# Cross-attention and mixture of experts: the second batch's last two tiles of the shared FFN, moved from in front of the experts to the stage of the gathers

## The chip, the cores and the metric

The kernel runs on one core of a Trainium2 chip. The metric is the device time of one launch in microseconds (us). All arithmetic is in fp32.

## The reference, cut to what matters

The input is 4 batches of 512 tokens with 512 features, so 2048 tokens, or 16 tiles of 128 tokens, 4 to a batch. A cross-attention block is added to the input; then comes a feed-forward block with 64 experts of which each token takes 6, and a shared feed-forward part that every token takes:

```
x = x + xattn(layernorm(x), context)
h = layernorm(x)
scores = softmax(h @ gate_w.T);  topk_w, topk_idx = top_k(scores, 6);  topk_w /= sum(topk_w)
# each expert takes up to 384 of the tokens sent to it
eo[e] = (silu(buf[e] @ w_gate[e].T) * (buf[e] @ w_up[e].T)) @ w_down[e].T      # 512 -> 352 -> 512
y[token] += topk_w * eo[expert, place]                                         # six rows a token
shared = (silu(h @ sh_gate.T) * (h @ sh_up.T)) @ sh_down.T                     # 512 -> 704 -> 512
out = x + y + shared
```

The change concerns `shared` and the sums over the six expert rows.

## The kernel before, in words

The result is kept in SBUF in `acc`, 16 tiles of 128 tokens by 512 features. The kernel runs in these stages, one after the other on TensorE:

1. Attention for the 16 tiles, with routing beside it. For every token the slots of its six expert rows go to `slot_get` and their weights to `top_w`. The normalised tokens go to DRAM twice, as rows (`h2_d`) and turned (`h2T_d`).
2. The shared FFN of batch 0 stands among the last routing steps of attention, with attention's buffers (`Here`).
3. The shared FFN of batch 1 follows in front of the experts, with the buffers of the later stages (`There`). Beside it the first experts' weights (`up_weights`, `down_weights`, issued by SyncE, called SP) and gathered tokens (`tokens`, issued by GpSimd, called POOL) are loaded.
4. 64 experts. The widths of the products depend on how many tokens an expert has (160, 192, 224, 256 or 384 columns; `kinds`, `by_width`). The results go to DRAM (`eo_d`).
5. The end: the shared FFN of batches 2 and 3 on TensorE, and beside it the sums. For each of 96 pairs of tile and rank, POOL gathers 128 rows of `eo_d` (`gather`, L873) and VectorE multiplies them by the weight and adds them to `acc` (`combine`, L884). A tile is written out (L865) when all has been added to it that is due in this stage (`added`, with its counter `left`).

`shared` is a generator: each `yield` ends a step, and the caller puts other work in between. Its first step loads the turned input of the batch into a slab (L122). Then come six slices of the 704 hidden features, five of 128 and one of 64. In a slice TensorE multiplies the gate's and the up's weights with the input (L128; the last slice has both in one product), ScalarE takes silu (L139) and VectorE multiplies (L140) into `hid`. A product over 512 features is four matmuls, and an fp32 matmul is two TensorE instructions in the trace, so a full slice has 16 and the last one 8. Then for each tile of the batch the down product (L145, twelve instructions) is added to `acc` (L148). There are eight slabs: six hold the shared weights, so two inputs fit at a time.

Products go to PSUM banks in pairs that are used in turn, `pg`, `pu`, `tx` and `pd`. The activations of the experts read a fixed 384 columns of a bank, also where the product wrote fewer.

In the end stage there are 12 buffers for gathered rows (`places`), so POOL can be 12 gathers ahead of the sums. The program's order fixes the rest: after each TensorE step of the shared FFN, VectorE's queue gets as many sums as bring the total to a share of 96, less a lag `behind` of 10 (5 after the last step; what is left then follows in a row). The share is counted in steps (`step` of `len(late) * slices`): six slices and four down tiles for each of two batches, 20 in all.

```
while done < NT * TOPK * step // (len(late) * slices) - (behind // 2 if last else behind):
    next(sums)
    done += 1
```

The order of PE, ACT, DVE and POOL instructions in the attention, expert and end stages is the program's order (`manual_schedule`); SP's order is arranged by the compiler.

Of the kernel before, what the change touches and what calls it, by code (L numbers as in the profile page):

```python
# [11 lines left out]
AF = mybir.ActivationFunctionType  # L12
ALU = mybir.AluOpType
AX = mybir.AxisListType

P = 128
B, S, D = 4, 512, 512
# [4 lines left out]
NT = B * S // P  # L22
TB = S // P
NC = D // P
E, F, TOPK = 64, 352, 6
# [6 lines left out]
FSC = [(i * P, min(P, FS - i * P)) for i in range((FS + P - 1) // P)]  # L32
# [1 line left out]
LN_EPS, QK_EPS = 1e-5, 1e-6  # L34
WIDTHS = (160, 192, 224, 256, CAP)
HALF = P // 2
BEFORE = 2
FAR = float(1 << 20)


# [1 line left out]
def xattn_moe_kernel(ctx, tc, a, out):  # L42
    nc = tc.nc
# [6 lines left out]
    h2T_d = dram.tile([D, B * S], F32, name="h2T_d")  # L50
# [3 lines left out]
    acc = keep.tile([P, NT, D], F32, name="acc")  # L54
# [40 lines left out]
    def slab(*shape):  # L95
        n = 1
        for m in shape:
            n *= m
        names = "abc"[:len(shape)]
        return slabs.tile([P, NC * D], F32, tag="slab", name="slab")[:, :n].rearrange(  # L100
            f"p ({' '.join(names)}) -> p {' '.join(names)}", **dict(zip(names, shape)))


    sh_gu, sh_down = [], []
# [10 lines left out]
            if full < 3:  # L115
                nc.sync.dma_start(sh_down[-1][:FS % P, full, :], a["sh_downT"][(f + full) * P:, :])

    def shared(b, get):


        xT = slab(NC, S)
        nc.sync.dma_start(xT, h2T_d.rearrange("(c p) n -> p c n", p=P)[:, :, b * S:(b + 1) * S])  # L122
        yield
        hid = [get.hid() for _ in range(0, len(FSC), 3)]

        def product(dst, w0):
            for c in range(NC):
                nc.tensor.matmul(dst, sh_gu[c][:, w0:w0 + P], xT[:, c, :], start=c == 0, stop=c == NC - 1)  # L128

        for fc, (f0, fn) in enumerate(FSC):  # L130
            pg, pu = get.pair()
            product(pg, f0)
            if fn == P:
                product(pu, FS + FS % P + f0)
            else:
                pu = pg[fn:]
            yield
            sg = get.sg()
            nc.scalar.activation(sg[:fn], pg[:fn], AF.Silu)  # L139
            nc.vector.tensor_tensor(hid[fc // 3][:fn, fc % 3, :], sg[:fn], pu[:fn], ALU.mult)  # L140
            yield
        for m in range(TB):
            pd = get.pd()
            for fc, (f0, fn) in enumerate(FSC):
                nc.tensor.matmul(pd, hid[fc // 3][:fn, fc % 3, m * P:(m + 1) * P], sh_down[fc // 3][:fn, fc % 3, :],  # L145
                                 start=fc == 0, stop=fc == len(FSC) - 1)
            t = b * TB + m
            nc.vector.tensor_tensor(acc[:, t, :], pd, acc[:, t, :], ALU.add)  # L148
            yield

    swp = ctx.enter_context(tc.tile_pool(name="swp", bufs=1))
# [4 lines left out]
    with ExitStack() as att:  # L156
# [425 lines left out]
        with tc.manual_schedule(engines=engines):  # L582
            new = scores(0, qTs[0], kvs[0][0])
            pr = w2.tile([P, NC, SC], F32, tag="pr", name="pr")
            for i in range(2):
                maximum(*new, i)
                exponentials(pr, *new, tail[0][2], 0, i)
            for u, (t, g) in enumerate(units):
                b, i = divmod(t, TB)
                pd, rd, sm = tail[t]  # L590
                if g == 0:
                    pc = ps_c.tile([P, NC, P], F32, tag="pc", name="pc")
                    if i == 2 and b + 2 < B:
                        load_batch(b + 2)
                    if t == NT - 2:
                        load_shared()
                mix_tail(pr, g, pd, rd, sm)
                if g == NC - 1:
                    wide = inverse_sums(sm)
                pr_u = pr  # L600
                if u + 1 < len(units):
                    tn, gn = units[u + 1]
                    new = scores(gn, qTs[tn], kvs[tn // TB][0])
                    pr = w2.tile([P, NC, SC], F32, tag="pr", name="pr")
                pT = [copied(turned(pr_u, c), nc.scalar) for c in range(2)]
                if u + 1 < len(units):
                    maximum(*new, 0)
                    maximum(*new, 1)
                    exponentials(pr, *new, tail[tn][2], gn, 0)
                beside()  # L610
                pT.append(copied(turned(pr_u, 2), nc.scalar))
                pT.append(copied(turned(pr_u, 3), nc.vector))
                if u + 1 < len(units):
                    exponentials(pr, *new, tail[tn][2], gn, 1)
                for c in range(2):
                    values(pc, g, c, pT[c], kvs[b][1])
                if g < NC - 1:
                    beside()
                for c in range(2, SC // P):
                    values(pc, g, c, pT[c], kvs[b][1])  # L620
                if g == NC - 1:
                    side.append(("finish", finish(t, pc, wide)))
                    beside()

            class Here:
                hid = staticmethod(lambda: w2.tile([P, NC, SC], F32, tag="pr", name="pr")[:, :3, :])
                sg = staticmethod(lambda: w2.tile([P, NC, P], F32, tag="pT", name="pT", bufs=5).rearrange(
                    "p a b -> p (a b)"))
                pair = staticmethod(lambda: (lambda ps: (ps[:, 0, :], ps[:, 1, :]))(
                    ps_s.tile([P, 2, SC], F32, tag="ps", name="ps")))  # L630
                pd = staticmethod(lambda: ps_s.tile([P, 2, SC], F32, tag="ps", name="ps")[:, 0, :])

            def advance(steps, n):
                for _ in range(n):
                    next(steps, None)

            (_, oldest), (_, older), (_, newer) = side
            advance(oldest, 1)
            work = shared(0, Here)
            next(work)  # L640

            for n_older, n_newer in ((5, 2), (4, 0), (0, 3), (0, 2), (0, 4), (0, 2)):
                next(work)
                advance(older, n_older)
                advance(newer, n_newer)
                next(work)
            advance(newer, 4)
            lists_made = plan()
            for _ in range(TB):
                next(lists_made, None)  # L650
                next(work)
            for steps in (oldest, older, newer, lists_made, work):
                assert next(steps, None) is None
# [6 lines left out]

    banks = {n: [psum.tile([P, 512], F32, name=f"{n}{i}") for i in range(2)] for n in ("pg", "pu", "tx", "pd")}
    turn = dict.fromkeys(banks, 0)

    def bank(name):
        turn[name] ^= 1
# [146 lines left out]
        nc.sync.dma_start(rows.rearrange("(m p) n -> p m n", p=P)[:, ::2, :], eo[:, ::2, :])  # L812
        yield

    others = {b: shared(b, There) for b in range(1, B)}
    next(others[1])
    held = up_weights(0)
    wd = down_weights(0)
    for b in range(1, BEFORE):
        for _ in others[b]:  # L820
            pass
    for b in range(BEFORE, B):
        next(others[b])
    kinds = [nc.values_load(kind_i[0:1, e:e + 1], engines=[PE], min_val=0, max_val=len(WIDTHS) - 1,
                            skip_runtime_bounds_check_because="a sum of len(WIDTHS) - 1 comparisons")
             for e in range(E)]
# [7 lines left out]
    with tc.manual_schedule(engines=engines):  # L834
# [22 lines left out]

        left = {t: TOPK + (t >= BEFORE * TB) for t in range(NT)}  # L860

        def added(t):
            left[t] -= 1
            if not left[t]:
                nc.sync.dma_start(out[t * P:(t + 1) * P, :], acc[:, t, :])  # L865
# [20 lines left out]
                added(t)  # L886
                yield

        late = range(BEFORE, B)
        whole = [t for b in range(BEFORE) for t in range(b * TB, (b + 1) * TB)]  # L890
        tiles = []
        for i, b in enumerate(late):
            tiles += whole[i * len(whole) // len(late):(i + 1) * len(whole) // len(late)] + list(
                range(b * TB, (b + 1) * TB))
        sums = combine([(t, k) for t in tiles for k in range(TOPK)])
        slices = len(FSC) + TB
        behind = len(places) - 2
        done = 0
        for i, b in enumerate(late):
            for n, _ in enumerate(others[b]):  # L900
                if n < 2 * len(FSC):
                    if n % 2 == 0:
                        continue
                    step = i * slices + n // 2 + 1
                else:
                    m = n - 2 * len(FSC)
                    added(b * TB + m)
                    step = i * slices + len(FSC) + m + 1
                last = step == len(late) * slices
                while done < NT * TOPK * step // (len(late) * slices) - (behind // 2 if last else behind):  # L910
                    next(sums)
                    done += 1
        for _ in sums:
            pass

# [47 lines left out]
```

## Time and profile before

| | |
|---|---|
| time, median of 3 runs (lowest to highest) | 1899.08 us (1897.15 to 1904.79) |
| the profiled execution: its own time, its span | 1896.93 us, 1895.1 us |
| granted TensorE clock, mean | 0.972 |
| busy: TensorE, VectorE, ScalarE, GpSimd | 1738.1, 852.3, 601.4, 677.7 us |
| batch 1's shared FFN on TensorE | 743.3 to 803.2 us |
| the experts on TensorE | 803.2 to 1748.2 us |
| the end: TensorE at work, then up to the last instruction | 1748.2 to 1868.5, to 1895.1 us |

The span is the time from the first to the last instruction of the profiled execution; its own time has a little around it. In the lines of the profile PE is TensorE's matmuls, PEld its weight loads (which lie beside matmuls), DVE VectorE, ACT ScalarE, POOL GpSimd, SP SyncE, and L128 is line 128 of the kernel. A group of instructions gives the line, the engine, the operation, the output and inputs by the program's names, the shape, the count, and then busy time and mean duration. A wait names who waited, for whom, and the total, the number and the longest of such waits in us. `slab` is the shared weights and inputs, `eo` in a shared line its hidden values, and `g` and `xg` in the end are the buffers of the gathered rows.

### The profile page before, as it was taken

The page shows a single profiled execution, that of the slowest core. Times are in us where ns is not written, and L with a number is a line of the kernel's source. Part 1 is how long each engine was busy: PE and PEld are TensorE (multiplying, and loading weights), DVE is VectorE, ACT ScalarE, POOL GpSimd, SP SyncE. Part 2 cuts the span into 40 slices and gives each one's busy share as a digit, 9 for nine tenths or more (in the row PEclk, how much of TensorE's full clock was granted, in tenths as well). Part 3 has the DMA queues.
Part 4 walks back from the last instruction along what each step waited for, and adds up shares of the span by engine and source line. Part 5 has one row for each costly group of instructions (what it writes and reads, how often), then busy time and mean ns, then how long its engine had stood idle before and what let it go on. Part 6 is the DMA issues. An engine that isn't in the chain of part 4 may idle for free.

```text
span 1895.1 us, 28083 instructions
## 1 busy us (share of the span) xinstructions
PE 1738.1 (92%) x10556; PEld 1134.2 (60%) x10556; DVE 852.3 (45%) x1656; ACT 601.4 (32%) x1326; POOL 677.7 (36%) x620
## 2 busy tenths in 40 slices
PE   4689998999899898999999999999999999999994
PEld 1255555555555543476767767777777777666441
DVE  4256777777777732132322333333333333222565
ACT  0155565556566620022222222222232222222000
POOL 5435666655755332021211111221212122110776
PEclk9789999999999999999999999999999999999997
DMA  7000000010110114166876777787888787755676
GB/s 252 2 7 20 21 16 18 18 33 12 43 55 26 46 34 142 40 225 229 264 231 233 254 241 268 255 275 269 277 283 288 263 270 266 232 198 161 185 229 207
DMA packets 122658, 302.62 MB, mean 160 GB/s; under 512 B 16560, under 2 KB 44496, under 8 KB 114224
## 3 DMA queue, kind: packets, MB, share of 16 engines
q1 hardware_dynamic: 94928, 220.76, 34.2%
q0 software_dynamic: 26400, 76.16, 13.2%
q8 instruction: 197, 3.23, 0.7%
q10 hardware_dynamic: 1088, 2.10, 0.3%
q14 instruction: 45, 0.37, 0.1%
HBM read 235.28 MB, written 63.55 MB: 158 GB/s over the span
## 4 chain that ended last, share of the span: by engine, by line
PE 74%; DVE 10%; POOL 9%; DMA 3%; issue 3%; ACT 2%; SPq 0%; POOLq 0%; DVEq 0%
PE pg L743 16%; PE pd L782 10%; PE pu L743 10%; PE pd L788 6%; PE mm L264 5%; DVE nm L357 4%; PE x L376 3%; PE tx L731 3%; PE pu L764 3%; PE pg L128 3%; POOL hn_r L251 3%; PE pu L128 3%; PE pc L387 2%; PE pd L145 2%; PE x L233 2%
## 5 line engine op out<-in xcount | busy, mean ns | idle before, releaser
L690 POOL DMA_INDIRECT xg<-h_d,lists x192 | 182.0, 948 | 790.5 <-PE tx L731 716.1
L743 PE MATMUL pg<-xT,wgu 128*128 128x192 f32 (+4 forms) x1536 | 320.2, 351 | 11.2 <-issue 10.8
L743 PEld LDWEIGHTS pg<-xT,wgu 128*128 128x128 f32 x1536 | 257.8, 190 | 77.9 <-issue 57.9
L755 DVE TENSOR_TENSOR ehid<-sg,pu 128x384 f32<-128x384 f32 x128 | 70.9, 554 | 452.1 <-PE pu L743 446.7
L782 PE MATMUL pd<-wd,ehid 128*128 128x512 f32 (+1 forms) x408 | 213.2, 609 | 0.7 <-ACT eo L811 0.7
L743 PE MATMUL pu<-xT,wgu 128*128 128x192 f32 (+4 forms) x1024 | 205.9, 344 | 0.0
L754 ACT ACTIVATE sg<-pg 128x384 f32<-128x384 f32 x128 | 62.9, 491 | 380.2 <-PE pg L743 380.2
L743 PEld LDWEIGHTS pu<-xT,wgu 128*128 128x128 f32 x1024 | 176.0, 191 | 12.2 <-issue 1.5
L361 ACT ACTIVATE pr<-ps,nm 128x496 f32<-128x496 f32 x256 | 171.0, 677 | 17.3 <-DVE nm L357 16.4
L376 PEld LDWEIGHTS x<-ident,pr 128*128 128x128 f32 x1024 | 116.4, 145 | 92.7 <-issue 60.0
L381 ACT COPY pT<-x 128x512 f32<-128x512 f32 x192 | 106.6, 586 | 194.6 <-PE x L376 192.7
L376 PE MATMUL x<-ident,pr 128*128 128x128 f32 x1024 | 147.1, 286 | 14.8 <-DVE r_hot L458 8.3
L357 DVE TENSOR_REDUCE nm<-ps 128x2 f32<-128x992 f32 x128 | 145.2, 1173 | 17.2 <-PE ps L351 17.1
L788 PE MATMUL pd<-wd,ehid 128*64 128x256 f32 x1092 | 131.3, 384 | 9.0 <-ACT uh L771 4.4
L251 POOL TENSOR_TENSOR hn_r<-hn_var,mhalf 128x16 f32<-128x16 f32 (+1 forms) x33 | 96.6, 2927 | 95.6 <-DVE hn_var L249 80.7
L733 DVE COPY xT<-tx 128x512 f32<-128x512 f32 x192 | 126.0, 685 | 3.6 <-PE tx L731 2.1
L477 POOL DMA_INDIRECT list_d<-token_id,r_put x96 | 100.5, 1047 | 27.4 <-issue 24.9
L769 DVE TENSOR_TENSOR ehid<-sg,pg 32x384 f32<-32x384 f32 x64 | 35.8, 559 | 162.4 <-ACT sg L768 162.4
L788 PEld LDWEIGHTS pd<-wd,ehid 128*64 128x64 f32 x1092 | 78.1, 138 | 48.1 <-issue 7.4
L387 PE MATMUL pc<-pT,slab 128*32 128x128 f32 x2048 | 86.1, 289 | 3.4 <-DVE pT L381 2.7
L387 PEld LDWEIGHTS pc<-pT,slab 128*32 128x32 f32 x2048 | 50.5, 113 | 50.9 <-issue 39.9
L873 POOL DMA_INDIRECT g<-eo_d,slot_get x48 | 51.9, 1081 | 78.1 <-issue 66.7
(161 smaller groups left out, 2363.6 us busy)
## 6 DMA issues: line engine op xcount, KB each, us to landing
wgu<-in_w_gu SPq DMA_DIRECT2D x64, 1408.0 KB, 6.9
wd<-in_w_down SPq DMA_DIRECT2D x64, 512.0 KB, 6.6
eo_d<-eo SPq DMA_DIRECT2D x64, 512.0 KB, 5.2
eo_d<-eo SPq DMA_DIRECT2D x128, 128.0 KB, 4.8
wd<-in_w_down SPq DMA_DIRECT2D x64, 192.0 KB, 6.7
acc<-in_x SPq DMA_DIRECT2D x16, 256.0 KB, 5.2
h_d<-h SPq DMA_DIRECT2D x16, 256.0 KB, 2.0
h2T_d<-hT SPq DMA_DIRECT2D x16, 256.0 KB, 2.3
```

The lines of the kernel that those rows point to most:

```text
L128: nc.tensor.matmul(dst, sh_gu[c][:, w0:w0 + P], xT[:, c, :], start=c == 0, stop=c == NC - 1)
L251: nc.gpsimd.tensor_tensor(r[:m], var[:m], mhalf[:m], ALU.pow)
L357: nc.vector.tensor_reduce(nm[:, 2 * i:2 * i + 2], pss[i][:, :, :SM], AX.X, ALU.max, negate=True)
L361: nc.scalar.activation(pr[:, r, :SM], pss[i][:, r % 2, :SM], AF.Exp, bias=nm[:, r:r + 1], accum_out=sm[:, g * NC + r:g * NC + r + 1])
L376: nc.tensor.transpose(tp[:, r, :], pr[:, r, c * P:(c + 1) * P], ident)
L381: (engine.copy if engine is nc.scalar else engine.tensor_copy)(pT, tp)
L387: nc.tensor.matmul(pc[r * HD:(r + 1) * HD, g, :], kv[:, c, h * HD:(h + 1) * HD], pT[:, r, :], start=c == 0, stop=c == SC // P - 1)
L690: nc.gpsimd.indirect_dma_start(out=x[:, :], out_offset=None, in_=h2_d[:, :], in_offset=bass.IndirectOffsetOnAxis(ap=lists[:, e * CT + c:e ...
L733: nc.vector.tensor_copy(xT[:, :, c * P:(c + 1) * P], tp)
L743: nc.tensor.matmul(dst[:, :n], wgu[:, c, w0:w0 + P], xT[:, c, :n], start=c == 0, stop=c == NC - 1)
L782: nc.tensor.matmul(pd, hid[:fn, fc, m * P:(m + 1) * P], wd[:fn, fc, :], start=fc == 0, stop=fc == len(FC) - 1)
L788: nc.tensor.matmul(pd[d * HALF:(d + 1) * HALF, i * D // 2:(i + 1) * D // 2], hid[:fn, fc, P + i * HALF:P + (i + 1) * HALF], wd[:fn, fc, d ...
```

## The change

The shared FFN is now done by parts, each a range of a batch's tiles: `(batch, first tile, end tile)`. In front of the experts stay batch 0 and the first two tiles of batch 1. The last two tiles of batch 1 become a third part of the end stage, behind batches 2 and 3. In a part of two tiles the gate and up products are 256 columns wide instead of 512; the number of instructions in them is the same for either width. The input of the third late part is loaded when the first late part is done.

The three pairs of banks that the shared FFN uses are set to zero before it, since a part of two tiles leaves half of `pg` and `pu` unwritten. The pace of the sums is counted in TensorE work (`work_in`, 680 units in all) instead of steps, and the tiles are summed in another order: first those which get no shared part in the end (0 to 5), then those of batches 2 and 3, then tiles 6 and 7.

```diff
-BEFORE = 2
+BEFORE = ((0, 0, TB), (1, 0, TB // 2))
+LATE = ((2, 0, TB), (3, 0, TB), (1, TB // 2, TB))
...
-    def shared(b, get):
-        xT = slab(NC, S)
-        nc.sync.dma_start(xT, h2T_d.rearrange("(c p) n -> p c n", p=P)[:, :, b * S:(b + 1) * S])
+    def shared(part, get):
+        b, first, end = part
+        t0, n = b * TB + first, (end - first) * P
+        xT = slab(NC, n)
+        nc.sync.dma_start(xT, h2T_d.rearrange("(c p) n -> p c n", p=P)[:, :, t0 * P:t0 * P + n])
...
-                nc.tensor.matmul(dst, sh_gu[c][:, w0:w0 + P], xT[:, c, :], start=c == 0, stop=c == NC - 1)
+                nc.tensor.matmul(dst[:, :n], sh_gu[c][:, w0:w0 + P], xT[:, c, :], start=c == 0, stop=c == NC - 1)
...
-            nc.scalar.activation(sg[:fn], pg[:fn], AF.Silu)
-            nc.vector.tensor_tensor(hid[fc // 3][:fn, fc % 3, :], sg[:fn], pu[:fn], ALU.mult)
+            nc.scalar.activation(sg[:fn, :n], pg[:fn, :n], AF.Silu)
+            nc.vector.tensor_tensor(hid[fc // 3][:fn, fc % 3, :n], sg[:fn, :n], pu[:fn, :n], ALU.mult)
...
-        for m in range(TB):
+        for m in range(end - first):
...
+    for n in ("pg", "pu", "pd"):
+        for dst in banks[n]:
+            nc.vector.memset(dst, 0.0)
...
-    others = {b: shared(b, There) for b in range(1, B)}
-    next(others[1])
+    rest_before = [shared(part, There) for part in BEFORE[1:]]
+    late = [shared(part, There) for part in LATE]
+    for work in rest_before:
+        next(work)
     held = up_weights(0)
     wd = down_weights(0)
-    for b in range(1, BEFORE):
-        for _ in others[b]:
+    for work in rest_before:
+        for _ in work:
             pass
-    for b in range(BEFORE, B):
-        next(others[b])
+    for work in late[:2]:
+        next(work)
...
-        left = {t: TOPK + (t >= BEFORE * TB) for t in range(NT)}
+        own = [[b * TB + m for m in range(first, end)] for b, first, end in LATE]
+        left = {t: TOPK + any(t in o for o in own) for t in range(NT)}
...
+        tiles = [t for t in range(NT) if left[t] == TOPK] + sum(own, [])
         sums = combine([(t, k) for t in tiles for k in range(TOPK)])
-        slices = len(FSC) + TB
         behind = len(places) - 2
+        work_in = [[len(o) * (2 if fn == P else 1) * NC for _, fn in FSC] + [len(FSC) * NC] * len(o) for o in own]
+        total, spent, done = sum(map(sum, work_in)), 0, 0
+        for i, (work, o) in enumerate(zip(late, own)):
+            for n, _ in enumerate(work):
                 if n < 2 * len(FSC):
                     if n % 2 == 0:
                         continue
-                    step = i * slices + n // 2 + 1
+                    spent += work_in[i][n // 2]
                 else:
                     m = n - 2 * len(FSC)
-                    added(b * TB + m)
-                    step = i * slices + len(FSC) + m + 1
-                last = step == len(late) * slices
-                while done < NT * TOPK * step // (len(late) * slices) - (behind // 2 if last else behind):
+                    added(o[m])
+                    spent += work_in[i][len(FSC) + m]
+                while done < NT * TOPK * spent // total - (behind // 2 if spent == total else behind):
                     next(sums)
                     done += 1
+            if i + 2 < len(late):
+                next(late[i + 2])
```

More of the change, by code (lines that the diff above doesn't have):

```diff
@@ L146, in shared @@
                                  start=fc == 0, stop=fc == len(FSC) - 1)
-            t = b * TB + m
-            nc.vector.tensor_tensor(acc[:, t, :], pd, acc[:, t, :], ALU.add)
+            nc.vector.tensor_tensor(acc[:, t0 + m, :], pd, acc[:, t0 + m, :], ALU.add)
             yield
@@ L638, in xattn_moe_kernel @@
             advance(oldest, 1)
-            work = shared(0, Here)
+            work = shared(BEFORE[0], Here)
             next(work)
@@ L887, in combine @@
                 yield
[L889 to L894, printed above, removed]
+        tiles = [t for t in range(NT) if left[t] == TOPK] + sum(own, [])
         sums = combine([(t, k) for t in tiles for k in range(TOPK)])
-        slices = len(FSC) + TB
         behind = len(places) - 2
-        done = 0
-        for i, b in enumerate(late):
-            for n, _ in enumerate(others[b]):
+        work_in = [[len(o) * (2 if fn == P else 1) * NC for _, fn in FSC] + [len(FSC) * NC] * len(o) for o in own]
+        total, spent, done = sum(map(sum, work_in)), 0, 0
+        for i, (work, o) in enumerate(zip(late, own)):
+            for n, _ in enumerate(work):
                 if n < 2 * len(FSC):
```

## The prediction

> **What bounds the kernel now.** I read the busy times first, then a table of stages, then the last stage's groups, chain and waits. Overall TensorE is the busiest engine by far, so only stages in which it stands still can give time back:
>
> ```profile
> PE 1738.1 (92%) x10556; PEld 1134.2 (60%) x10556; DVE 852.3 (45%) x1656; ACT 601.4 (32%) x1326; POOL 677.7 (36%) x620
> ```
>
> The stages that the change touches, from the windows of time (length, then busy time and count of PE, PEld, DVE, ACT, POOL; granted clock, DMA share, GB/s). The first row is the second batch's shared FFN in front of the experts, the next two are batches 2 and 3 with the gathers, the last is what follows TensorE's last instruction:
>
> ```profile
> 743.00:803.20 60.20, 59.95 (x137) 25.18 (x137) 6.40 (x10) 3.58 (x6) 5.78 (x6) 1.00 0.33 116
> 1748.20:1808.00 59.80, 59.80 (x138) 25.25 (x136) 30.03 (x42) 4.36 (x8) 39.44 (x38) 1.00 0.65 191
> 1808.00:1868.60 60.60, 60.50 (x138) 25.17 (x136) 39.96 (x56) 3.58 (x6) 47.19 (x45) 1.00 0.76 223
> 1868.60:1895.10 26.50, 0.00 (x0) 0.00 (x0) 13.50 (x18) 0.00 (x0) 14.83 (x15) 0.53 0.66 198
> ```
>
> To see here: TensorE is full in all three FFN stages, some 60 us a batch, and then stands for 26.5 us while the sums finish. Those 26.5 us are all that the change can shorten. The end of the chain and the waits of the last stage say what fills them:
>
> ```profile
> 1874.60 4.60 DMA g<-eo_d,slot_get
> 1879.24 0.94 POOL g L873
> ...
> 1886.75 3.95 DMA xg<-eo_d,slot_get
> 1890.79 0.75 DVE acc L884
> ```
>
> (start, length, what), and of the waits from 1748 on (total, times, longest):
>
> ```profile
> DVE acc L884 <- DMA xg<-eo_d,slot_get: 7.7, 10, 1.5
> DVE acc L884 <- DMA g<-eo_d,slot_get: 6.5, 7, 1.4
> ```
>
> The chain alternates between POOL's gathers and their landing, and VectorE waits 14.2 us for rows. POOL issues 96 gathers from 1753.83 to 1886.75, 1.40 us from one to the next (132.9 / 95), and TensorE has 120 us of work for them: 1.25 us a gather. POOL is the slower of the two, so it is late when TensorE ends.
>
> **What the Trainium skill says.** "TensorE: Matmul & The Clock Gate", Back-to-back issue gap: the distance between matmuls is set by the weight load and the matmul together. The trace agrees that the load is covered at both widths needed here: 190 ns of load inside 0.429 us at 512 columns, and 0.215 us at 256 columns, from the timeline of an expert (start, length, what):
>
> ```profile
> 822.47 1.89 PE L743 MATMUL pu<-xT,wgu 128*128 128x256 f32 x8
> 824.19 1.02 PE L782 MATMUL pd<-wd,ehid 128*128 128x512 f32 x2
> ```
>
> Eight in 1.72 us from start to start are 0.215 us each. "SBUF — State Buffer", Who interferes with whom: a VectorE instruction with two SBUF inputs contends with a GpSimd instruction that reads SBUF. The sums are of that kind; gathers last 0.95 us alone and up to 1.45 us beside them, which fits but doesn't prove it. I use only POOL's mean pace, which has it inside.
>
> **Part 1, the second batch's half leaves the front.** A batch is 88 TensorE instructions of gate and up (5 slices of 16, one of 8) and 4 tiles of down. 88 x 0.429 = 37.8 us; a down tile takes 5.54 us (from one acc add to the next, 786.67 to 792.21); 37.8 + 4 x 5.54 = 59.9 us, as the first window shows. With two tiles the 88 stay but are half as wide, 88 x 0.215 = 18.9 us, and two down tiles go: 18.9 + 11.1 = 30.0 us remain. **Gain 29.9 us.** This stage also covers the loads of experts 0 and 1, and their gathers. The windows show them done:
>
> ```profile
> 758.00:763.00 5.00, 5.00 (x13) 2.23 (x12) 0.05 (x1) 0.60 (x1) 0.00 (x0) 1.00 0.43 167
> 763.00:768.00 5.00, 5.00 (x13) 2.27 (x12) 0.69 (x1) 0.41 (x1) 0.00 (x0) 1.00 0.00 0
> ```
>
> The traffic ends by 763; expert 0 would now start at about 774.5, so that cover keeps some 11 us. SP: batch 3's input load waits for a slab that is free once the half's gate-ups are done (743.3 + 18.9 = 762 instead of 781); it blocks SP for less time than now, and the next load behind it isn't due before expert 0 frees its weights. Cost nothing.
>
> **Part 2, six memsets of PSUM banks.** The trace has no such instruction. TensorE's first product there already waits for the last VectorE add of the attention stage:
>
> ```profile
> 743.25 3.70 PE L128 MATMUL pg<-slab 128*128 128x512 f32 x8 [0.78 <-DVE acc L148]
> ```
>
> The memsets stand behind that add in VectorE's order, and the first bank used is pg1, the second cleared. "VectorE: DVE Perf Modes", Zero memsets can be issued as uint32, has a memset at one cycle per element, which at its 0.96 GHz makes my estimate 0.53 us for 512 columns; the nearest row, a 512-column add from PSUM (L148), takes 0.69. I take 0.6: 2 x 0.6 = **1.2 us of loss**. The other four are needed later (pu1 3.4 us on) and hide under the first products. Bounds: 0 if they run in the 4.8 us in which VectorE idles before that add, 6 x 0.69 = 4.1 us if TensorE waits for all. Nothing excludes the lower one, nothing makes it a gain.
>
> **Part 3, the half comes back at the end.** 88 x 0.215 + 11.1 = **30.0 us more TensorE** behind batch 3. ACT gets 6 activations and VectorE 6 products and 2 adds with it, all beside it: VectorE's whole work in the end is about 96 x 0.785 = 75 us for the sums, 12 x 0.69 for the old products, 6 at half that, and 10 adds x 0.69, 93 us in 150. Its queue: between two products stand 2 or 3 sums (2.4 us) where a 256-wide slice takes 3.4 us, so no bank is held. The half's input is one more load of 512 KB on SP, issued after batch 2 into a slab freed 22 us earlier, landing in about 5 us and needed a batch (60 us) later. It stands behind output writes of finished tiles only. No cost. Where the hidden buffers change hands, VectorE has the last add and three sums (3.1 us) before the half's first product, and TensorE is then still in its first slice. POOL keeps its 96 gathers.
>
> **Part 4, the pace.** The sums are now spread over 680 units of TensorE work. By hand: 82 sums are due before the last down tile, 9 after it and 5 at the very end, so 14 follow the last add (15 before: 81, 10 and 5). With 150 us of TensorE work a gather is due every 1.56 us against POOL's 1.40: gather 94 is possible at 5.6 + 93 x 1.40 + 4.5 = 140 us after the stage's start, before TensorE ends at 150. The last two gathers wait for buffers of sums 83 and 84, and land some 6 us later, while eleven sums (8.6 us) still stand before theirs. So the rows are there, and the tail is VectorE's alone: 0.1 + 0.72 for the add + 14 x 0.785 (four sums in 3.11 us, 0.785 from start to start) + 3.6 from the last sum to the end of the output write, as now (1891.54 to 1895.1) = 15.4 us. Of the 26.5 us this leaves out 3.25 (the last add, ready at 1868.6, runs at 1871.85), 7.2 (15 sums and the add take 19.7 us instead of 12.5) and one sum: **gain 11.2 us**. What is late next is VectorE's own run of 14 sums.
>
> **Sum.** -29.9 + 1.2 + 30.0 - 11.2 = -9.9 us, so the profiled span goes from 1895.1 to about 1885, its own time from 1896.9 to 1887. The median of the runs shown, 1899.1, stands 2.2 us above that execution; from it: 1889. About 0.5%, 9.5 us, is what can be told from no change here, so the forecast lies right on that line.
>
> **Rivals.** *A, as worked out*: 1889, with the memset bounds and a sum or two either way 1886 to 1893. *B, the tail stays*: POOL remains the bound, because its pace sinks with the demand (a gather that waits for a buffer starts late). For it: single distances of 1.6 to 1.7 us in the last third. Against it: the clean distance is 1.25, and the lead of 12 gathers is 18 us of work. Then -29.9 + 1.2 + 30.0 is left: 1900, no change. *C, slower: the weight load shows at 256 columns.* Twice 88 instructions now carry as many loads for half the columns. If the 190 ns stood beside the 0.215, they would cost 176 x 0.19 = 33 us, giving 1922; it decides from 9.9 / 176 = 0.056 us each, a distance of 0.27 us. Against it: the expert's 0.215 us at the same shape; for it only that those runs are 8 long. *D, the change does only half*: the memsets cost the full 4.1 us and half the waits for rows stay, -1.5 to -5: 1895.
>
> **How the numbers follow.** A 0.7, B 0.12, D 0.09, C 0.09. Within A's own range and the spread of a median (about 2 us) some seven in ten fall beyond 9.5 us: faster 0.5, same 0.4 (the rest of A with B and D), slower 0.1 (C and a little of B). The range runs from A's best with that spread, 1884, to B with it, 1902; C lies outside.
>
> **What would show it.** Right: 88 more matmul instructions (10644), six memsets, one more input load; expert 0 near 774.5; 30 us of 256-wide work at 0.215 before TensorE ends; VectorE's waits for gathered rows near zero in the end; 15 us from TensorE's last instruction to the end. Wrong: rows still awaited after TensorE ends (B), a distance above 0.27 us (C), TensorE idle at 743 for over 2 us or between batch 3 and the half.

## The result, and the profile after

The median goes from 1904.36 us (20 runs, 1897.15 to 1915.1) to 1894.65 us (20 runs, 1890.58 to 1900.09). The ratio is 0.9949, with a 95% interval of 0.9936 to 0.9962: 9.7 us less. The forecast was 9.9 us less and 1889 us; the kernel before, over more runs, lies 5.3 us above its first three, so the changed kernel's own median lies 5.7 us above the forecast, inside the range. The very same kernel, run again beside other experiments, gave 0.9959 (0.9942 to 0.9976).

The profiled execution after has a span of 1893.5 us and an own time of 1895.29 us, only 1.6 us under the one before. Read alone, that would be no change, so I read the stages first. "Attention ends" is the last add of the attention stage; "front" runs from there to expert 0's first transpose; "end" from the first late product to the last instruction. The third and fourth rows are the two kernels run again (us, from the traces).

| kernel | attention ends | front | experts | end, TensorE | end, after TensorE |
|---|---|---|---|---|---|
| before | 743.2 | 60.0 | 945.5 | 119.8 | 26.7 |
| after | 751.3 | 30.8 | 946.6 | 149.9 | 14.8 |
| before again | 743.9 | 60.0 | 937.5 | 119.8 | 26.8 |
| after again | 744.3 | 32.5 | 946.3 | 149.9 | 14.8 |

The two stages that the change touches repeat to 0.1 us at the end and 1.7 us in front. Attention and the experts run the same instructions in both and wander by 8 to 9 us from one execution to the next, whichever kernel it is. So the effect is read from the stages: front -29.2, end +18.2, together -11.0 us (-9.3 with the front of the second execution), which agrees with the timed ratio's 9.7.

The busy times after, to set beside those of before:

```profile
PE 1743.1 (92%) x10644; PEld 1153.7 (61%) x10644; DVE 854.4 (45%) x1668; ACT 601.0 (32%) x1332; POOL 678.3 (36%) x620
```

There are the 88 more matmul instructions, 12 more on VectorE (six memsets and six products) and six more activations. The windows by stage, columns as before: front, batch 2, batch 3, the half, and what follows TensorE's last instruction:

```profile
751.30:782.10 30.80, 30.02 (x112) 20.95 (x112) 6.14 (x14) 2.29 (x6) 5.76 (x6) 1.00 0.64 226
1728.70:1788.50 59.80, 59.80 (x137) 25.06 (x135) 24.18 (x34) 4.16 (x7) 37.32 (x36) 1.00 0.63 185
1788.50:1848.50 60.00, 60.00 (x137) 25.17 (x136) 34.10 (x48) 3.58 (x6) 42.40 (x40) 1.00 0.68 202
1848.50:1878.70 30.20, 30.15 (x113) 20.95 (x112) 17.45 (x28) 2.29 (x6) 20.78 (x20) 1.00 0.66 192
1878.70:1893.50 14.80, 0.00 (x0) 0.00 (x0) 10.94 (x15) 0.00 (x0) 2.48 (x2) 0.58 0.36 121
```

TensorE is full in all of the first four: the half costs 30 us where it now stands and gave back 30 us where it stood. The last row is shorter by 12 us. The end's timeline says why:

```profile
1865.88 1.89 PE L131 MATMUL pg<-slab 128*128 128x256 f32 x8
1867.60 11.05 PE L148 MATMUL pd<-slab,eo 128*128 128x512 f32 x24
1878.69 0.69 DVE L150 TENSOR_TENSOR acc<-pd,acc 128x512 f32<-128x512 f32 x1 [2.56 <-PE pd L148]
1879.30 1.53 DVE L892 SCALAR_TENSOR_TENSOR acc<-xg,top_w,acc 128x512 f32<-128x512 f32 x2
1880.74 4.68 DVE L892 SCALAR_TENSOR_TENSOR acc<-g,top_w,acc 128x512 f32<-128x512 f32 x6
1885.35 4.68 DVE L892 SCALAR_TENSOR_TENSOR acc<-xg,top_w,acc 128x512 f32<-128x512 f32 x6
```

VectorE waits 2.56 us for TensorE's last product, adds it, and then has its 14 sums in a row with no wait. Before, the same add ran 3.25 us late and rows were awaited after it. In the waits from 1728 on, no line has the sums waiting for a DMA any more (nor in the second execution); the wait has changed sides:

```profile
POOL g L881 <- DVE acc L892: 18.3, 18, 3.3
...
POOL xg L881 <- DVE acc L892: 7.5, 15, 1.6
```

POOL now waits for VectorE to give buffers back, 25.8 us in all. The last row is asked for 7.3 us before its sum:

```profile
1881.95 1.15 POOL L881 DMA_INDIRECT xg<-eo_d,slot_get  x1 [0.30 <-issue]
```

Its sum is the one at 1889.28 below. Before, 4.0 us lay between the two (1886.75 and 1890.79), where a landing took 3.9 us in the median. The chain's end, which alternated between gathers and landings, is now one gather and then only sums, with no gap that a DMA fills:

```profile
1877.72 3.04 DMA xg<-eo_d,slot_get
1880.76 0.74 DVE acc L892
...
1881.53 0.76 DVE acc L892
...
1889.28 0.75 DVE acc L892
```

The gather that the chain still names is not what the sums wait for. Rows are gathered and summed in the same order, and the one asked for at 1877.72, third from the end, belongs to the sum at 1887.70.

### The profile page after: what moved, and what is told of

Its sections match the earlier page's. It is cut to its first block, busy times and chain, and to the rows that moved or that the text cites. A ratio compares the mean times of both kernels' runs of the same rounds, so it can differ in the third digit from the quotient of the medians.

```text
span 1893.5 us, 28291 instructions
## 1 busy us (share of the span) xinstructions
PE 1743.1 (92%) x10644; PEld 1153.7 (61%) x10644; DVE 854.4 (45%) x1668; ACT 601.0 (32%) x1332; POOL 678.3 (36%) x620
## 4 chain that ended last, share of the span: by engine, by line
PE 76%; DVE 10%; POOL 8%; issue 3%; DMA 2%; ACT 2%; another core or an unknown queue 0%; SPq 0%; POOLq 0%; DVEq 0%
PE pg L748 16%; PE pd L787 10%; PE pu L748 10%; PE pd L793 6%; PE mm L266 5%; DVE nm L359 4%; PE x L378 3%; PE pg L131 3%; PE pd L148 3%; PE tx L736 3%; PE pu L769 3%; PE pu L131 3%; POOL hn_r L253 3%; PE pc L389 2%; PE x L235 2%
```

## The experiments

My theory: TensorE's work is moved at no price, and the gain is the tail that POOL's gathers made, since 150 us of TensorE work cover 96 gathers and 120 us do not. Rivals: the new pace and order of the sums alone bring the gain; the lag kept behind TensorE, not POOL, was what the tail cost before; and more TensorE work at the end goes on helping. Unless another base is named, each edit is against the changed kernel, and each ratio is against the kernel before on the same chip. Two chips were used, on which the medians of the kernel before were 1903.54 and 1905.11 us on the one and 1892.15 on the other, so times from different chips can't be compared. The ratios are those on record; the quotient of two medians differs from them by up to 0.002.

**The pace alone, with the old split.**

```diff
-BEFORE = ((0, 0, TB), (1, 0, TB // 2))
-LATE = ((2, 0, TB), (3, 0, TB), (1, TB // 2, TB))
+BEFORE = ((0, 0, TB), (1, 0, TB))
+LATE = ((2, 0, TB), (3, 0, TB))
```

> The old split (batch 1 whole in front, batches 2 and 3 late) with everything else of the change: pace by TensorE work, new order of the tiles, memsets. My theory (the gain is POOL's late rows, which only more TensorE work in the end covers): the end stays bound by POOL, last instruction 145 to 147 us after the stage's first product, TensorE's end to the last instruction 25 to 27 us, waits of L892 for gathered rows still 10 us or more; time against the kernel before 0 to +1 us, ratio 0.999 to 1.001. Rival (the new pace and order did it, the place of the half did nothing): tail near 15 us, about -10 us, ratio 0.995.

Measured: 1905.22 us over 22 runs, ratio 0.9999 (0.9988 to 1.0011). The rival that the pace alone brings the gain falls. The profile is not the one I expected, though: the sums wait for rows for only 0.4 us, and the tail is 16.2 us. What the tail lost came up elsewhere, in TensorE, by the waits from 1728 on:

```profile
PE pd L148 <- DVE eo L143: 11.3, 2, 8.0
```

TensorE stood for VectorE's late products, and the end took 151.7 us, against 146.5 before. In that timeline ScalarE and VectorE begin their part of the last two slices 11 to 16 us after the recorded end of TensorE's products:

```profile
1843.63 3.60 PE L131 MATMUL pg<-slab 128*128 128x512 f32 x8
1847.07 3.60 PE L131 MATMUL pu<-slab 128*128 128x512 f32 x8
...
1858.35 0.60 ACT L142 ACTIVATE sg<-pg 128x512 f32<-128x512 f32 x1 [14.83 <-PE pd L148]
...
1864.81 0.69 DVE L143 TENSOR_TENSOR eo<-sg,pu 128x512 f32<-128x512 f32 x1 [12.30 <-remote]
```

Why, the trace doesn't show. So the time speaks against the rival, but this profile is no clean proof of POOL's part.

**A lag that shrinks to zero.** Without the 14 sums behind the last add the tail should shrink, if it is VectorE's.

```diff
-                while done < NT * TOPK * spent // total - (behind // 2 if spent == total else behind):
+                while done < NT * TOPK * spent // total - behind * (total - spent) // total:
```

> The changed kernel with a lag that falls from 10 sums at the stage's start to 0 at its end, so that 4 instead of 14 sums follow the last add. TensorE's order is the same. My theory (after the change the rows are there and the tail is VectorE's own run of sums): tail 0.1 + 0.72 + 4 x 0.785 + 3.6 = 7.6 us instead of 14.9, so 7 us under the changed kernel, some -17 us against the kernel before, ratio 0.991. Rival (POOL is still as slow as TensorE there): sums wait for rows, tail stays at 12 us or more, no more than 3 us under the changed kernel, ratio 0.994 or above.

Measured: 1892.55 us (6 runs), ratio 0.9931 (0.9912 to 0.9949). The tail was 7.3 us, as worked out: an add, four sums, an output write. Of the 7 us that this saves, some 3.4 showed in the ratio, and the two intervals overlap. In the profile TensorE stood for 5 us in the last slices (2.68 and 2.35):

```profile
1870.60 3.60 PE L148 MATMUL pd<-slab,eo 128*128 128x512 f32 x8
...
1875.98 0.64 ACT L142 ACTIVATE sg<-pg 128x256 f32<-128x256 f32 x2 [8.14 <-remote]
...
1876.87 1.12 PE L148 MATMUL pd<-slab,eo 128*128 128x512 f32 x2 [2.68 <-DVE eo L143]
```

The down product waits for VectorE's product, which waits for ScalarE, which starts 8.7 us after the recorded end of the product that it reads (1867.30). This profiled execution, at 1899.08 us, was the slowest of the six; the other five took 1891.34 to 1892.7, so the stand may be its own.

**The same lag with the old split.** If the lag was the cost before, this must win as well. Both edits above together:

```diff
+BEFORE = ((0, 0, TB), (1, 0, TB))
+LATE = ((2, 0, TB), (3, 0, TB))
...
+                while done < NT * TOPK * spent // total - behind * (total - spent) // total:
```

> The falling lag with the old split (batch 1 whole in front). My theory: POOL's 96 gathers at 1.4 us bound the end, so a shorter lag only makes VectorE wait earlier: last instruction still 145 to 148 us after the stage's first product, ratio 0.999 to 1.002; sums in front of products may hold TensorE a little. Rival (the lag alone was the cost before as well): tail near 8 us, -15 us or more, ratio 0.992.

Measured: 1906.37 us (22 runs), ratio 1.0017 (1.0001 to 1.0032). The waits of its end stage:

```profile
DVE acc L892 <- DMA xg<-eo_d,slot_get: 10.3, 12, 1.5
DVE acc L892 <- DMA g<-eo_d,slot_get: 9.0, 11, 1.9
```

and, of the same view from 1728 on, what stood behind those sums:

```profile
PE pd L148 <- DVE acc L150: 10.5, 2, 9.8
```

The sums are asked for sooner than the rows come: 19.3 us of waits, and TensorE's down products wait 10.5 us for adds of VectorE that follow the sums in its queue. The tail is 8.3 us, but the end takes 157.6, where I had expected 145 to 148. The lag as the cause before falls.

**One rank fewer to gather, in the kernel before.** This takes gathers away and leaves TensorE's work as it was. The sixth row of every token is left out of the sum.

```diff
-        left = {t: TOPK + (t >= BEFORE * TB) for t in range(NT)}
+        left = {t: TOPK - 1 + (t >= BEFORE * TB) for t in range(NT)}
...
+        sums = combine([(t, k) for t in tiles for k in range(TOPK - 1)])
...
-                while done < NT * TOPK * step // (len(late) * slices) - (behind // 2 if last else behind):
+                while done < NT * (TOPK - 1) * step // (len(late) * slices) - (behind // 2 if last else behind):
```

> The kernel before with only five of the six expert rows gathered and summed in the end (80 gathers and sums instead of 96; the sixth row of every token is left out). It takes work from POOL and VectorE and leaves TensorE's as it was. My theory (POOL's pace of 1.4 us a gather is what makes the tail of before): 80 x 1.40 = 112 us fit under TensorE's 120, so the rows are there and the tail becomes VectorE's run of 14 sums, 15 us instead of 26.7; end stage 135 us instead of 146.5, ratio about 0.994. Rival (the tail is VectorE's work or the lag of the program's order, not the rows): the same number of sums follows TensorE's end as before (14 against 15), so it stays at 25 us and the ratio at 0.999.

Measured: 1890.85 us (4 runs), ratio 0.9911 (0.9885 to 0.9937). Its end stage, up to TensorE's end and after it:

```profile
1755.40:1875.20 119.80, 119.80 (x273) 50.21 (x271) 60.33 (x85) 7.74 (x13) 80.30 (x75) 1.00 0.66 194
1875.20:1890.30 15.10, 0.01 (x1) 0.00 (x0) 10.95 (x15) 0.00 (x0) 6.08 (x6) 0.66 0.58 183
```

With 80 gathers instead of 96 beside the same 120 us, a sum never waits for a row, and the tail is 15.1 us, with the same 15 VectorE instructions, an add and 14 sums, as after the change. Split, lag and pace are those of before; only the number of pairs to gather and sum is smaller. VectorE loses 16 sums too, but it had 14.2 us of waits for rows, not a lack of time. That the gathers made the tail is shown here; POOL's issue and the landing of the rows were taken away together, so their shares are not told apart. The end stage is 11.6 us shorter, as worked out. The ratio says some 17 us (12 to 22), where I had expected 0.994; what lies beyond the end stage stays open.

**How many tiles to move.** All four, one, and three of batch 1's tiles at the end:

```diff
+BEFORE = ((0, 0, TB),)
+LATE = ((2, 0, TB), (3, 0, TB), (1, 0, TB))
```

> All four tiles of batch 1 late, nothing of it in front of the experts. My theory (the half that stays in front covers the loads of experts 0 and 1; the tail gains nothing more, since it is VectorE's already): TensorE idles 11 to 14 us in front of expert 0's first transposes (rows and weights land about 10 us after the attention stage), tail 15 us, so 12 us over the changed kernel, ratio to before 1.000 to 1.002. Rival (the cover is worth nothing): TensorE idles under 3 us, same as the changed kernel, ratio 0.995. Second rival (POOL was still late after the change, more TensorE work in the end helps again): below the changed kernel, ratio 0.993 or less.

```diff
+BEFORE = ((0, 0, TB), (1, 0, 3))
+LATE = ((2, 0, TB), (3, 0, TB), (1, 3, TB))
```

> Three tiles of batch 1 in front, one late (the change has two and two). My theory: TensorE's work in the end 120 + 88 x 0.13 to 0.14 + 5.5 = 137 us (128-wide products can't be faster than the transposes' 0.13 us), three tiles in front 88 x 0.322 + 3 x 5.54 = 45 us; the rows are possible at 143 us, so the tail is 15 to 17 us and the last instruction 152 to 154 us after the stage's first product. Against before -15 + 0.7 + 6 to 8 = -6 to -8 us, ratio 0.996. Rival (only half of POOL's lateness is covered by a quarter): tail 21 us or more, ratio 0.998 or above.

```diff
+BEFORE = ((0, 0, TB), (1, 0, 1))
+LATE = ((2, 0, TB), (3, 0, TB), (1, 1, TB))
```

> One tile of batch 1 in front, three late. My theory: the tail is VectorE's already with two late tiles, so nothing more is gained there: 14 to 15 us; one tile in front takes 17 us (128-wide at 0.13), and the loads of expert 0 land about 11 us after the attention stage, so they stay covered and those of expert 1 barely; end stage 120 + 45 + 15 = 180 us. Against before -43 + 0.7 + 33.5 = -8.5 us, ratio 0.9955, like the change and like three tiles in front. Rival (the cover is short by several us): experts start later, ratio 0.998 or above.

| tiles moved | ratio (interval) | front | end | after TensorE |
|---|---|---|---|---|
| 1 | 0.9955 (0.9935 to 0.9974) | 45.7 | 150.0 | 14.8 |
| 2, the change | 0.9949 (0.9936 to 0.9962) | 30.8 | 164.7 | 14.8 |
| 3 | 0.9944 (0.9925 to 0.9963) | 17.7 | 179.7 | 14.8 |
| 4 | 0.9972 (0.996 to 0.9983) | 6.8 | 193.6 | 13.8 |

One, two and three can't be told apart. Fifteen us more of TensorE work are enough to let POOL be ahead at the end; after that a tile costs at the end what it saves in front, and the tail stays at 14.8. With all four nothing covers expert 0's loads any more, as TensorE's timeline at the start of the experts shows:

```profile
758.04 1.08 PE L736 MATMUL tx<-ident,xg 128*128 128x128 f32 x4 [7.55 <-issue]
760.08 1.12 PE L736 MATMUL tx<-ident,xg 128*128 128x128 f32 x4 [0.95 <-DMA xg<-h_d,lists]
763.79 0.37 PE L737 MATMUL tx<-ident,xg 128*32 128x128 f32 x1 [2.60 <-DMA xg<-h_d,lists]
764.32 2.90 PE L748 MATMUL pg<-xT,wgu 128*128 128x192 f32 x8 [0.16 <-issue]
```

TensorE stands for 11 us there. My expectation had the direction and overdid the size: 4.4 us worse than the change by the ratios, where it had 12. By the traces, expert 0's first product starts 13.1 us after attention's end instead of 32.9, and the end is 28.9 us longer: 9.1 us worse. What lies between 9.1 and 4.4 stays open; the experts stage wanders by more than that. The rival that more TensorE work goes on helping falls: past one tile it brings nothing that can be told, and with all four it costs.

**The memsets narrow.** Only the columns that a part of two tiles leaves unwritten, up to the 384 that are read, and not `pd`:

```diff
-    for n in ("pg", "pu", "pd"):
+    for n in ("pg", "pu"):
         for dst in banks[n]:
-            nc.vector.memset(dst, 0.0)
+            nc.vector.memset(dst[:, TB // 2 * P:CAP], 0.0)
```

> The changed kernel with memsets of only columns 256 to 383 of pg and pu. My theory: TensorE's wait in front of its first product goes from 1.50 us to about 1.1 or below, and the stretch of half clock that followed the wait in three of six profiles with full memsets doesn't follow; half in front 30.5 us instead of 30.8 to 32.5. Too little to see in the time: ratio 0.993 to 0.996. Rival (the wait isn't the memsets'): 1.50 us again.

Measured: 1896.01 us (7 runs), ratio 0.9944 (0.9921 to 0.9966), which can't be told from the change. What it does is seen in the wait of the first product: 1.50 us after the change, 1.10 here, 0.78 before. The front is 30.4 us, against 30.8 and 32.5.

**The two kernels once more,** for the attention stage, which in the first profile after ended 8.1 us later than before.

> The changed kernel once more, for a second profile. My theory: stage by stage as in the first one, half in front 30 us, 150 us of TensorE work in the end without gaps, 15 us after it; the attention stage (the same code as before) ends anywhere from 743 to 752 us with the number of 3.4 us stretches at half clock. Rival (the change made the attention stage longer): it ends at 751 or later again. Ratio 0.995.

> The kernel before once more, one look for a second profile. My theory: attention stage ends at 750 us or so where the first profile had 743 (its time was at the low end of the runs), end stage 146 to 152 us from its first product, 25 us or more after TensorE's end or gaps in TensorE before it. Rival (the change lengthened the attention stage): it ends at 743 to 745 us again.

The changed kernel gave 1885.85 us (13 runs; the ratio is in the first section), the kernel before 1889.79 us in the one run made for this profile and 1892.15 in the median of 21 runs beside it. Attention ended at 744.3 and 743.9. I had expected some 750 for the kernel before and missed, but the two agree with each other: the 8 us of the first pair aren't the change's.

**The best version.** The tail that is left is 14 sums by the program's order. Here the sums are counted one down tile ahead and the lag shrinks to zero, so that all 96 stand before the last add; the memsets are the narrow ones.

```diff
-                while done < NT * TOPK * spent // total - (behind // 2 if spent == total else behind):
+                while done < NT * TOPK * min(spent + len(FSC) * NC, total) // total - behind * (total - spent) // total:
```

> The changed kernel with the lag falling to 0 before the last down tile (all 96 sums stand in front of the last add), and with memsets of only columns 256 to 383 of pg and pu, the ones that the experts read and a 256-wide product leaves unwritten (four memsets of 128 columns, and none that TensorE's first products overlap). My theory: TensorE's end to the last instruction 0.1 + 0.7 + 3.6 = 4.4 us, first product 0.7 us earlier after the attention stage: -11 us against the changed kernel where TensorE isn't held, ratio to before 0.989. In the profile of the falling lag alone VectorE's products came late in the last slices and TensorE stood 5 us there, so a part of it may go: 0.989 to 0.992. Rival (VectorE's sums in front of products hold TensorE by as much as the tail gets shorter): 0.994 to 0.996, with TensorE gaps of 5 us or more in the last 30 us.

Measured: 1875.85 us (6 runs), ratio 0.9896 (0.987 to 0.9922), at least twice the gain of the change. Its front, its end under TensorE and what follows:

```profile
740.40:770.90 30.50, 30.10 (x113) 21.00 (x113) 3.85 (x12) 2.30 (x6) 5.76 (x6) 1.00 0.64 229
1726.00:1875.90 149.90, 149.87 (x385) 71.13 (x383) 86.07 (x123) 10.04 (x19) 103.32 (x96) 1.00 0.69 203
1875.90:1880.10 4.20, 0.00 (x0) 0.00 (x0) 0.69 (x1) 0.00 (x0) 0.00 (x0) 0.68 0.17 64
```

All 96 gathers and sums fit under TensorE's 149.9 us without a gap in it, and one add and an output write are left. The late products of the shrinking lag above don't appear here, with sums queued even earlier. But this version ran on the other chip, so that doesn't clear early sums of having caused them.

## Why the prediction was right

- **The moved work.** Forecast 29.9 us out and 30.0 back. The front's TensorE is 30.0 us in the window, the end's grew by 30.1 (119.8 to 149.9). The 256-column instructions come at 0.216 us, eight in 1.73 (1862.42, 1864.15, 1865.88 in the timeline), so rival C, a weight load that shows, falls.
- **The cover in front.** Forecast as enough. The front's TensorE has no gap, and it is enough even with one tile less (17.7 us of front); with none it isn't.
- **The memsets.** The mis-sized term: forecast 1.2 us, measured 0.72. Each pair takes 1.03 us, near the two times 0.53 of the forecast's estimate, and the first product waits 1.50 us instead of 0.78:

```profile
751.50 1.02 DVE L667 MEMSET pg<- 128x512 f32 x2 [0.18 <-DVE acc L150]
752.09 2.83 PE L131 MATMUL pg<-slab 128*128 128x256 f32 x12 [1.50 <-issue]
752.58 1.03 DVE L667 MEMSET pu<- 128x512 f32 x2
```

  They stand behind the add, as forecast, not in the idle time in front of it. But the product starts at 752.09, before the pair ends at 752.52: it waited for one memset of the pair and not, as the forecast had it, for two. What I didn't foresee is a further 1.7 us in some executions, told below. With it, the changed kernel's second execution has a front of 32.5.
- **The tail.** Forecast 15.4 us, measured 14.8: add 0.69, 14 sums, 3.5 of output. POOL is out of it, by the waits after; that the gathers had made the tail before, the experiment with five ranks shows. Rival B falls with both, and D with the stage table, since no wait for rows is left and the memsets cost 0.7. The forecast put "late next" on VectorE's run of sums; removing it took the tail to 4.2.
- **The sum.** Forecast -9.9; the stages give -11.0 and -9.3, the runs -9.7. That the two agree to 0.2 us is luck, since the interval alone is 2.5 us wide on either side and the memset term was off by 0.5 and the tail by 0.6. The whole interval lies below 1, so the kernel is faster; whether by more than the 0.5% that the forecast gave as the line, the interval leaves open, as forecast. The absolute number was 5.7 us low, 5.3 of it because three runs had put the kernel before too low.
- **Expert 0's start.** Forecast near 774.5, seen at 782.1 in the first profile and 776.8 in the second. The forecast took attention's end as fixed; it isn't. Counted from that end it was 31.3 us, and 30.8 and 32.5 were seen.

## What to carry to other kernels

When an engine that feeds the end is slower than the work that covers it, move covering work there from a place with cover to spare; the whole gain is the tail, and it is used up as soon as the feeder is ahead. Then look at what the program's own order still leaves behind the last product: here that was as much again. Read such a change from the stages that it touches, since stages with unchanged code wandered by as much as it was worth.

## What the hardware showed unasked

**Half clock after a short wait.** In the changed kernel's second execution, the same wait of 1.50 us is followed by twelve instructions that take 4.51 us instead of 2.83:

```profile
745.11 4.51 PE L131 MATMUL pg<-slab 128*128 128x256 f32 x12 [1.50 <-issue]
```

and the windows of its first 3.4 us, and of the whole first 6.9 us, show the granted clock (the third value from the end):

```profile
745.11:748.50 3.39, 3.39 (x9) 2.80 (x10) 2.38 (x5) 0.00 (x0) 2.48 (x4) 0.57 0.91 365
745.11:752.00 6.89, 6.89 (x24) 5.79 (x25) 2.80 (x6) 0.38 (x1) 5.15 (x6) 0.75 0.97 354
```

The Trainium skill's "TensorE: Matmul & The Clock Gate", What's actually happening, has half clock after an idle window of about 3.4 us, full clock after about as long of work, and windows that run free, so that the count of slow instructions differs from run to run. The length of the stretch agrees. The wait doesn't: a stretch of half clock followed a wait of only 1.50 us in four of the seven profiles that have it before a product. The other three had none, nor did the profiles with waits of 0.78 (kernel before, twice, and with five rows) and 1.10 us (narrow memsets, two). With so few profiles this is a correlation; that the wait is the cause isn't shown.

**The attention stage drifts with such stretches.** Between 110 and 720 us I counted 6 of them in the kernel before (attention ends at 743.2), 8 after (751.3), 5 in both when run again (744.3, 743.9), 3 in the best version (740.4) and 9 with the narrow memsets alone (751.7). That they set the drift is a correlation; no run tested it, and the runs again and the best version were on one chip, the narrow memsets on the other.

**Narrow products come faster than one recorded load lasts.** With one tile moved, eight 128-column instructions come in 0.89 us, 0.112 each, against the 0.13 that I had assumed. Each has its weight load, which the trace records with 0.19 us, so the loads overlap in the record, and those 0.19 us are not the least distance between two:

```profile
1851.29 0.97 PEld L131 LDWEIGHTS pg<-slab 128*128 128x128 f32 x8
1851.40 1.06 PE L131 MATMUL pg<-slab 128*128 128x128 f32 x8
...
1852.30 1.06 PE L131 MATMUL pu<-slab 128*128 128x128 f32 x8
```

**Left open:** why ScalarE and VectorE start their part of a slice up to 16 us after TensorE's recorded end in three kernels of this study (the pace alone and the two with the shrinking lag alone), and at most 2.6 us after it in the others. The kernel alone doesn't decide it: the changed kernel has 2.6 us in its first profile and at most 1.1 in its second. All three ran on one chip. Every profile from that chip lacks some of the engines' semaphore records (in the pace alone VectorE has 1417 for 1578 instructions), and those from the other lack none. So the profile itself may have a part in these late starts, in what it records or in the execution that it records.
